# GRU, attention and AUGRU on one core: five shrinking softmax blocks, two products moved from VectorE to GpSimd, attention matmuls ahead of the next gates, first loads reordered

## The chip, the cores and the metric

The kernel runs on one core of a Trainium2 chip. The metric is device time in microseconds (us) of that core, the median of several executions. "Faster" or "slower" is said of a difference above 2%.

## The reference

A recommender scores 1024 users. Each has 100 history items of 128 numbers. A GRU runs over the history, an attention network scores each GRU state against the candidate item, the softmax of the scores pools the states, and the pooled vector (its element t, not a score) weights step t of a second recurrence, the AUGRU. A small network predicts from its last state and other features.

```python
h_new = (1 - z) * n + z * h                     # GRU, 100 steps; keys = all states
feat  = concat([keys, q, keys - q, q * keys])   # q: the item's embedding
score = mlp(feat)                               # 512 -> 80 -> 40 -> 1, relu
attn  = softmax(where(mask == 1, score, -inf), over the 100 steps)
pooled = einsum('bt,btd->bd', attn, keys)
# AUGRU over the keys: u = pooled[:, t] * sigmoid(...), h = (1 - u) * h + u * h_hat
# cut: history sum, predictor
```

## The kernel before

The batch is cut into two halves of 512 columns; half 1 runs five steps ("ticks") behind half 0. A tile is 128 x 512 in fp32 (256 KB). A step of a half has six gate matmuls and three for the attention (three layers, working on three different steps); the profile shows two instructions for each, 18 in all. Scores are collected row by row; at the end of a block (`ENDS`) the softmax of the block is made, and the rows of that block can be pooled: a row is one step's weights broadcast over the partitions, `eb`, times the key tile `k`, added to `pooled`.

```python
ENDS = (48, 92, T)
# gates of step t: matmuls into PSUM, then a chain on VectorE and ScalarE
nc.vector.scalar_tensor_tensor(out=u, in0=ph, scalar=bhh[:, 2:3], in1=r, op0=ALU.add, op1=ALU.mult)
nc.vector.tensor_add(pi, pi, u)
nc.scalar.activation(pi, pi, AF.Tanh, bias=bih[:, 2:3])
nc.vector.tensor_sub(d, h if t else h0, pi)
nc.vector.tensor_mul(d, pz, d)
nc.vector.tensor_add(hn, pi, d)                 # the new state
nc.gpsimd.tensor_mul(m, x, m)                   # history sum, on GpSimd
nc.gpsimd.tensor_add(hist[:, cols], hist[:, cols], m)
nc.sync.dma_start(out=keys_d[t][:, cols], in_=hn)
# ... attend(t): three pairs of matmuls
nc.vector.tensor_mul(kq, self.h, item[:, self.cols])
# ... pm = wk.h + wkq.kq + w12.mv, then f = pm + q0, mv = relu(f)
# ... pool(count): for each row
eb = kp.tile([P, HB], F32, name="eb")           # kp: 4 buffers of each tile
nc.sync.dma_start(out=eb, in_=e_d[j][row, self.cols].partition_broadcast(P))
k = kp.tile([P, HB], F32, name="k")
nc.sync.dma_start(out=k, in_=keys_d[t][:, self.cols])
nc.vector.tensor_mul(eb, k, eb)                 # the pooling product
nc.vector.tensor_add(acc, acc, eb)              # the sum; acc = pooled[:, cols], in SBUF
# ... the loop over ticks
for half, s in now:
    if 0 <= s < T: half.gru(s)                  # AUGRU steps from T + GAP on: cut
for half, s in now:
    if 0 <= s < T:
        half.attend(s)
        half.pool(2 if len(half.todo) > T - s else 1)
```

All big loads go through one queue (SyncE's). In PSUM the kernel keeps six tiles for gates (`ps`) and two for attention (`pa`); each is called a bank here. Independent instructions are reordered before they reach an engine, so the order on an engine isn't the program's.

## Time and profile before

| | before |
|---|---|
| median of 3 runs | 2873.81 us (2870.04 to 2875.78) |
| profiled span, granted clock | 2876.6 us, 0.972 |
| TensorE / VectorE / GpSimd busy | 93% / 64% / 28% |
| pooling sums: number, mean | 198, 767 ns |

The page's first part gives busy time of each engine; its second cuts the span into 40 slices and gives the busy tenths of each (9 is 90% or more).

```profile
PE 2669.4 (93%) x6080; PEld 1150.3 (40%) x6080; DVE 1843.4 (64%) x2674; ACT 945.5 (33%) x1431; POOL 809.9 (28%) x615
...
PE   6999999999999988999998847499999999999998
...
DVE  4666666666678998766666988655555555555553
...
POOL 3333333333333332333332300022222222222221
```

TensorE (PE) has three weak places: the first slice, two slices of 8 where VectorE (DVE) is at 9, and the hole of 8, 8, 4, 7, 4. The hole is the turn, where GRU and pooling end and the AUGRU begins.

To compare kernels I cut the span into five stages and count TensorE's instructions. The view below gives, for each stretch, its length, then busy us and (instructions) of TensorE, its weight loads, VectorE, ScalarE and GpSimd, then granted clock, DMA share and GB/s.

```profile
0.00:80.00 80.00, 56.55 (x106) 22.60 (x106) 39.11 (x56) 18.47 (x28) 30.25 (x35) 0.89 0.58 185
80.00:720.00 640.00, 620.83 (x1424) 267.38 (x1425) 412.69 (x556) 205.70 (x317) 214.74 (x159) 1.00 0.30 98
720.00:1520.00 800.00, 761.93 (x1732) 324.81 (x1731) 602.78 (x857) 252.26 (x388) 264.83 (x190) 0.99 0.48 152
1520.00:1920.00 400.00, 280.78 (x619) 118.70 (x618) 302.30 (x481) 99.81 (x150) 70.28 (x52) 0.85 0.65 206
1920.00:2870.00 950.00, 946.38 (x2199) 416.40 (x2198) 486.54 (x726) 367.68 (x549) 229.84 (x181) 1.00 0.31 98
```

At the full pitch of 0.429 us an instruction, **lost time** of a stage is its length minus 0.429 x its instructions: start 80 - 106 x 0.429 = 35 us, steady GRU 29, softmax and pooling stages (720 to 1520) 57, turn (1520 to 1920) 134. This measure is used throughout. It is not idle time alone: where instructions take longer than the pitch, that counts as lost too.

### The profile page before, as it was taken

What the parts mean: (1) busy time and instruction counts of PE and PEld (TensorE: products, weight loads), DVE (VectorE), ACT (ScalarE), POOL (GpSimd) and SP (SyncE); (2) the same over time, 40 slices, a digit from 0 to 9 for tenths busy, and PEclk for the clock granted to TensorE, in tenths of its full rate; (3) what the DMA queues carried; (4) which work ended last, traced back from release to release, by engine and by line L of the source; (5) the groups of instructions that cost most, each with busy time, mean ns of one, the idle gap of its engine ahead of it and who ended that gap; (6) DMA issues with size and microseconds to landing.
All of it is one profiled execution on the core that took longest, in us unless ns stands there. A gap on an engine that the chain in (4) does not pass through costs nothing.

```text
span 2876.6 us, 22338 instructions
## 1 busy us (share of the span) xinstructions
PE 2669.4 (93%) x6080; PEld 1150.3 (40%) x6080; DVE 1843.4 (64%) x2674; ACT 945.5 (33%) x1431; POOL 809.9 (28%) x615
## 2 busy tenths in 40 slices
PE   6999999999999988999998847499999999999998
PEld 2444444444434333444443312144444444444443
DVE  4666666666678998766666988655555555555553
ACT  2333333333333222333333312133333333333333
POOL 3333333333333332333332300022222222222221
PEclk8999999999999999999999978699999999999999
DMA  6332323222245777433334777733333333333331
GB/s 196 99 99 95 103 95 103 93 99 99 96 135 188 236 240 224 158 100 102 106 100 134 237 237 253 227 102 103 102 103 102 102 102 102 102 102 102 103 101 42
DMA packets 213650, 375.69 MB, mean 131 GB/s; under 512 B 31568, under 2 KB 32436, under 8 KB 213524
## 3 DMA queue, kind: packets, MB, share of 16 engines
q1 hardware_dynamic: 213524, 374.27, 40.9%
q8 instruction: 47, 0.77, 0.1%
q14 instruction: 79, 0.65, 0.1%
HBM read 320.08 MB, written 53.67 MB: 130 GB/s over the span
## 4 chain that ended last, share of the span: by engine, by line
PE 64%; DVE 20%; DMA 8%; issue 5%; ACT 3%; SPq 1%; POOL 1%; DVEq 0%; ACTq 0%; POOLq 0%
PE ps L189 18%; PE pm L237 10%; PE pu L348 6%; PE pr L348 6%; PE ph L348 6%; PE pr L350 6%; PE ph L350 6%; PE pu L350 6%; DVE d L218 3%; DMA k<-keys_d 3%; DVE hn L219 3%; DVE eb L318 3%; DMA eb<-e_d 3%; DVE u L209 2%; DVE d L217 2%
## 5 line engine op out<-in xcount | busy, mean ns | idle before, releaser
L189 PE MATMUL ps<-x,wih 128*128 128x512 f32 x1200 | 586.9, 597 | 0.0
L189 PE MATMUL ps<-hn,whh 128*128 128x512 f32 x1188 | 584.3, 599 | 1.8 <-DVE hn L219 1.8
L220 POOL TENSOR_TENSOR m<-x,m 128x512 f32<-128x512 f32 x200 | 262.7, 1313 | 1085.9 <-DMA x<-in_hist_x 1054.3
L362 POOL TENSOR_TENSOR u<-u,at 128x512 f32<-128x512 f32 x200 | 254.3, 1272 | 877.1 <-ACT u L361 865.1
L366 DVE TENSOR_TENSOR ph<-ph,hn 128x512 f32<-128x512 f32 x198 | 138.4, 699 | 450.5 <-ACT ph L364 450.3
L189 PEld LDWEIGHTS ps<-x,wih 128*128 128x128 f32 x1200 | 230.1, 192 | 291.3 <-issue 282.2
L189 PEld LDWEIGHTS ps<-hn,whh 128*128 128x128 f32 x1188 | 228.3, 192 | 289.9 <-issue 286.9
L237 PE MATMUL pm<-hn,wk 128*128 128x512 f32 x400 | 219.7, 632 | 95.0 <-DVE hn L219 94.8
L243 ACT ACTIVATE mv<-f 128x512 f32<-128x512 f32 x204 | 128.5, 630 | 540.9 <-DVE f L241 531.6
L221 POOL TENSOR_TENSOR hist<-hist,m 128x512 f32<-128x512 f32 x200 | 287.6, 1438 | 15.7
L215 ACT ACTIVATE ps<-ps,bih 128x512 f32<-128x512 f32 x200 | 132.4, 662 | 423.1 <-DVE ps L214 423.0
L348 PE MATMUL pr<-k,wr 128*128 128x512 f32 x396 | 203.4, 595 | 46.6 <-DMA k<-keys_d 46.6
L209 DVE SCALAR_TENSOR_TENSOR u<-ps,bhh,r 128x512 f32<-128x512 f32 x198 | 147.5, 745 | 144.6 <-PE ps L189 138.0
L237 PE MATMUL pm<-kq,wkq 128*128 128x512 f32 x400 | 216.5, 624 | 11.6 <-DVE kq L231 11.0
L241 DVE TENSOR_TENSOR f<-pm,q 128x512 f32<-128x512 f32 x204 | 139.7, 685 | 132.2 <-PE pm L237 132.0
L357 ACT ACTIVATE pr<-pr,br 128x512 f32<-128x512 f32 x198 | 131.1, 662 | 276.1 <-PE pr L350 276.1
L237 PE MATMUL pm<-mv,w 128*128 128x512 f32 x404 | 210.8, 604 | 2.6 <-ACT mv L243 2.6
L350 PE MATMUL pr<-hn,wr 128*128 128x512 f32 x396 | 204.1, 597 | 9.1 <-DVE hn L368 9.1
L217 DVE TENSOR_TENSOR d<-hn,ps 128x512 f32<-128x512 f32 x198 | 135.6, 685 | 115.1 <-ACT ps L215 115.1
L361 ACT ACTIVATE u<-pu,bu 128x512 f32<-128x512 f32 x200 | 137.3, 687 | 214.6 <-PE pu L350 214.6
L348 PE MATMUL pu<-k,wu 128*128 128x512 f32 x400 | 205.2, 594 | 0.0
L350 PE MATMUL ph<-r,wh 128*128 128x512 f32 x396 | 202.7, 593 | 2.4 <-DVE r L358 2.4
(93 smaller groups left out, 2936.5 us busy)
## 6 DMA issues: line engine op xcount, KB each, us to landing
k<-keys_d SPq DMA_DIRECT2D x400, 256.0 KB
eb<-e_d SPq DMA_DIRECT2D x206, 256.0 KB
x<-in_hist_x SPq DMA_DIRECT2D x200, 256.0 KB
m<-mask_d SPq DMA_DIRECT2D x200, 256.0 KB
keys_d<-hn SPq DMA_DIRECT2D x200, 256.0 KB
at<-att_d SPq DMA_DIRECT2D x200, 256.0 KB
s_b<-mv SPq DMA_DIRECT2D x200, 2.0 KB
item<-in_item SPq DMA_DIRECT2D x1, 512.0 KB
```

Source lines behind the costliest of these rows:

```text
L189: nc.tensor.matmul(p, lhsT=w[:, g, :], rhs=v, start=(n == 0), stop=(n == len(parts) - 1),)
L209: nc.vector.scalar_tensor_tensor(out=u, in0=ph, scalar=bhh[:, 2:3], in1=r, op0=ALU.add, op1=ALU.mult)
L217: nc.vector.tensor_sub(d, h if t else h0, pi)
L220: nc.gpsimd.tensor_mul(m, x, m)
L221: nc.gpsimd.tensor_add(hist[:, cols], hist[:, cols], m)
L237: nc.tensor.matmul(p, lhsT=w, rhs=v, start=(n == 0), stop=(n == len(parts) - 1))
L241: nc.vector.tensor_add(f, p, q0[:, self.cols])
L348: nc.tensor.matmul(p, lhsT=w[:, 1, :], rhs=k, start=True, stop=v is None)
L350: nc.tensor.matmul(p, lhsT=w[:, 0, :], rhs=v, start=False, stop=True)
L361: nc.scalar.activation(u, pu, AF.Sigmoid, bias=later["bu"])
L362: nc.gpsimd.tensor_mul(u, u, at)
L366: nc.vector.tensor_sub(ph, ph, h)
```

## The change

The intent: more, shrinking blocks so that few rows are left for the turn; the rows spread evenly; VectorE relieved of two products; each state used later, so that TensorE need not wait for it; an earlier start.

```diff
-ENDS = (48, 92, T)
+ENDS = (44, 72, 88, 96, T)
 # first loads: x of step 0 goes second in the queue, whh behind the biases
+    x_first = xp.tile([P, HB], F32, name="x")
+    nc.sync.dma_start(out=x_first, in_=a["hist_x"][0][:, :HB])
 # buffers: xp 5 -> 6, kp 4 -> 5
 # the two reciprocals of 128x512 become one of 128x8, through DRAM
-                nc.vector.tensor_mul(kq, self.h, item[:, self.cols])
+                nc.gpsimd.tensor_mul(kq, self.h, item[:, self.cols])
-                    nc.vector.tensor_mul(eb, k, eb)
+                    nc.gpsimd.tensor_mul(eb, k, eb)
                     nc.vector.tensor_add(acc, acc, eb)
 # the loop: attention of the step before, then the gates, half by half
-        for half, s in now: ... half.gru(s)
-        for half, s in now: ... half.attend(s)
-                half.pool(2 if len(half.todo) > T - s else 1)
+        for half in halves:
+            if 1 <= s <= T:
+                half.attend(s - 1)
+            if 0 <= s < T:
+                half.gru(s, parts)
+                left = next(e for e in ENDS if e > s - 2) - s + 2
+                half.pool(-(-len(half.todo) // left))
 # cut: functions split so that a step could be done in parts (it is done in one)
```

More of the change, by code (lines that the diff above doesn't have):

```diff
@@ L65 @@
     att_d = dram.tile([T, B], F32, name="att_d")
+    rlen_d = dram.tile([P, NG], F32, name="rlen_d")
     def load(name, shape, src=None, dt=F32):
@@ L73 @@
     wih = load("wih", [P, 3, P])
-    whh = load("whh", [P, 3, P])
+    xp = ctx.enter_context(tc.tile_pool(name="xp", bufs=6))
+    x_first = xp.tile([P, HB], F32, name="x")
+    nc.sync.dma_start(out=x_first, in_=a["hist_x"][0][:, :HB])
     bih = load("bih", [P, 3])
     bhh = load("bhh", [P, 3])
+    whh = load("whh", [P, 3, P])
     pre = ctx.enter_context(tc.tile_pool(name="pre", bufs=1))
@@ L120 @@
     y = const.tile([1, B], F32, name="y")
-    xp = ctx.enter_context(tc.tile_pool(name="xp", bufs=5))
     hp = ctx.enter_context(tc.tile_pool(name="hp", bufs=8))
@@ L125 @@
     sp = ctx.enter_context(tc.tile_pool(name="sp", bufs=2))
-    kp = ctx.enter_context(tc.tile_pool(name="kp", bufs=4))
+    kp = ctx.enter_context(tc.tile_pool(name="kp", bufs=5))
     ps = ctx.enter_context(tc.tile_pool(name="ps", bufs=6, space=PSUM))
@@ L159, in load_later @@
             later[n] = load(n, shape)
-        len_i = pre.tile([P, B], I32, name="len_i", tag="once2")
-        nc.sync.dma_start(out=len_i, in_=a["len_i"].partition_broadcast(P))
-        length = const.tile([P, B], F32, name="length")
+        len_i = pre.tile([T, B], I32, name="len_i", tag="once2")
+        nc.sync.dma_start(out=len_i, in_=a["len_i"].partition_broadcast(T))
+        length = const.tile([T, B], F32, name="length")
         nc.vector.tensor_copy(length, len_i)
         later["length"] = length
+        len_g = pre.tile([P, NG], I32, name="len_g")
+        nc.sync.dma_start(out=len_g, in_=a["len_i"].rearrange("(p g) -> p g", p=P))
+        rlen_g = pre.tile([P, NG], F32, name="rlen_g")
+        nc.vector.tensor_copy(rlen_g, len_g)
+        nc.vector.reciprocal(rlen_g, rlen_g)
+        nc.sync.dma_start(out=rlen_d, in_=rlen_g)
     class Half:
@@ L174, in __init__, with gru @@
             self.todo = []
-        def gru(self, t):
+        def gru(self, t, parts):
             cols = self.cols
-            x = xp.tile([P, HB], F32, name="x")
-            nc.sync.dma_start(out=x, in_=a["hist_x"][t][:, cols])
+            if t or self.i:
+                x = xp.tile([P, HB], F32, name="x")
+                nc.sync.dma_start(out=x, in_=a["hist_x"][t][:, cols])
+            else:
+                x = x_first
             m = xp.tile([P, HB], F32, name="m")
@@ L184, in gru, with gru_chain @@
             hn = hp.tile([P, HB], F32, tag="h", name="hn")
+            for c in parts:
+                self.gru_chain(t, x[:, c], h[:, c] if t else h0[:, c], hn[:, c])
+            nc.gpsimd.tensor_mul(m, x, m)
+            nc.gpsimd.tensor_add(hist[:, cols], hist[:, cols], m)
+            nc.sync.dma_start(out=keys_d[t][:, cols], in_=hn)
+            self.h = hn
+        def gru_chain(self, t, x, h, hn):
+            n = x.shape[-1]
             def gate(g, parts):
-                p = ps.tile([P, HB], F32, tag="g", name=f"ps{g}")
-                for n, (w, v) in enumerate(parts):
+                p = ps.tile([P, n], F32, tag="g", name=f"ps{g}")
+                for j, (w, v) in enumerate(parts):
                     nc.tensor.matmul(
@@ L192, in gate @@
                         rhs=v,
-                        start=(n == 0),
-                        stop=(n == len(parts) - 1),
+                        start=(j == 0),
+                        stop=(j == len(parts) - 1),
                     )
@@ L199, in gru @@
             pr = gate(0, both)
-            r = wp.tile([P, HB], F32, name="r")
+            r = wp.tile([P, n], F32, tag="r", name="r")
             nc.scalar.activation(r, pr, AF.Sigmoid, bias=brz[:, 0:1])
@@ L206, in gru @@
             nc.scalar.activation(pz, pz, AF.Sigmoid, bias=brz[:, 1:2])
-            u = wp.tile([P, HB], F32, name="u")
+            u = wp.tile([P, n], F32, tag="u", name="u")
             if t:
@@ L215, in gru @@
             nc.scalar.activation(pi, pi, AF.Tanh, bias=bih[:, 2:3])
-            d = wp.tile([P, HB], F32, name="d")
-            nc.vector.tensor_sub(d, h if t else h0, pi)
+            d = wp.tile([P, n], F32, tag="d", name="d")
+            nc.vector.tensor_sub(d, h, pi)
             nc.vector.tensor_mul(d, pz, d)
             nc.vector.tensor_add(hn, pi, d)
-            nc.gpsimd.tensor_mul(m, x, m)
-            nc.gpsimd.tensor_add(hist[:, cols], hist[:, cols], m)
-            nc.sync.dma_start(out=keys_d[t][:, cols], in_=hn)
-            self.h = hn
         def attend(self, t):
@@ L326, in weights @@
                 out=att,
-                in0=later["length"][:T, self.cols],
+                in0=later["length"][:, self.cols],
                 scalar=step[:T, :],
@@ L333, in weights, with augru, augru_chain @@
             nc.sync.dma_start(out=att_d[:, self.cols], in_=att)
-        def augru(self, t):
+        def augru(self, t, parts):
             cols = self.cols
-            wr, wu, wh = later["wr"], later["wu"], later["wh"]
-            at = kp.tile([P, HB], F32, name="at")
-            nc.sync.dma_start(out=at, in_=att_d[t, cols].partition_broadcast(P))
-            k = kp.tile([P, HB], F32, name="k3")
-            nc.sync.dma_start(out=k, in_=keys_d[t][:, cols])
-            h = self.h if t else None
-            hn = hp.tile([P, HB], F32, tag="h", name="hn3")
+            at = kp.tile([P, HB], F32, name="at", bufs=4)
+            nc.sync.dma_start(out=at, in_=att_d[t, cols].partition_broadcast(P))
+            k = kp.tile([P, HB], F32, name="k3", bufs=4)
+            nc.sync.dma_start(out=k, in_=keys_d[t][:, cols])
+            hn = hp.tile([P, HB], F32, tag="h", name="hn3")
+            for c in parts:
+                h = self.h[:, c] if t else None
+                self.augru_chain(k[:, c], at[:, c], h, hn[:, c])
+            self.h = hn
+        def augru_chain(self, k, at, h, hn):
+            wr, wu, wh = later["wr"], later["wu"], later["wh"]
+            n = k.shape[-1]
             def gate(w, v, name):
-                p = ps.tile([P, HB], F32, tag="g", name=name)
+                p = ps.tile([P, n], F32, tag="g", name=name)
                 nc.tensor.matmul(p, lhsT=w[:, 1, :], rhs=k, start=True, stop=v is None)
@@ L353, in augru @@
             r = None
-            if t:
+            if h is not None:
                 pr = gate(wr, h, "pr")
-                r = wp.tile([P, HB], F32, tag="r", name="r3")
+                r = wp.tile([P, n], F32, tag="r", name="r3")
                 nc.scalar.activation(pr, pr, AF.Sigmoid, bias=later["br"])
@@ L359, in augru @@
             pu = gate(wu, h, "pu")
-            u = wp.tile([P, HB], F32, tag="u", name="u3")
+            u = wp.tile([P, n], F32, tag="u", name="u3")
             nc.scalar.activation(u, pu, AF.Sigmoid, bias=later["bu"])
@@ L364, in augru @@
             nc.scalar.activation(ph, ph, AF.Tanh, bias=later["bh"])
-            if t:
+            if h is not None:
                 nc.vector.tensor_sub(ph, ph, h)
@@ L370, in augru @@
                 nc.vector.tensor_mul(hn, u, ph)
-            self.h = hn
         def features(self):
             cols = self.cols
-            rlen = wp.tile([P, HB], F32, name="rlen")
-            nc.vector.reciprocal(rlen, later["length"][:, cols])
-            nc.vector.tensor_mul(hist[:, cols], hist[:, cols], rlen)
+            rlen = kp.tile([P, HB], F32, tag="eb", name="rlen")
+            nc.sync.dma_start(
+                out=rlen,
+                in_=rlen_d.rearrange("p g -> (p g)")[cols].partition_broadcast(P),
+            )
+            nc.gpsimd.tensor_mul(hist[:, cols], hist[:, cols], rlen)
             cross = const.tile([P, HB], F32, name=f"cross{self.i}")
@@ L423, in predict @@
             )
+    parts = (ts(0, HB),)
     halves = [Half(i) for i in range(NH)]
-    for tick in range(2 * T + GAP + LAG):
+    for tick in range(2 * T + GAP + LAG + 1):
         if tick == 2:
             load_later()
-        now = [(half, tick - LAG * half.i) for half in halves]
-        for half, s in now:
-            if 0 <= s < T:
-                half.gru(s)
-            elif T + GAP <= s < 2 * T + GAP:
-                half.augru(s - T - GAP)
-        for half, s in now:
-            if 0 <= s < T:
-                half.attend(s)
-                half.pool(2 if len(half.todo) > T - s else 1)
-            elif s == T:
+        for half in halves:
+            s = tick - LAG * half.i
+            if 1 <= s <= T:
+                half.attend(s - 1)
+            if s == T:
                 half.attend(T)
                 half.attend(T + 1)
+            if 0 <= s < T:
+                half.gru(s, parts)
+            elif T + GAP <= s < 2 * T + GAP:
+                half.augru(s - T - GAP, parts)
+            if 0 <= s < T:
+                left = next(e for e in ENDS if e > s - 2) - s + 2
+                half.pool(-(-len(half.todo) // left))
+            elif s == T:
                 half.pool(len(half.todo))
@@ L445 @@
                 half.features()
-            elif s == 2 * T + GAP - 1:
+            elif s == 2 * T + GAP:
                 half.predict()
```

## The prediction

> **What bounds the kernel now.** I read the page's first two parts, then busy time by stage, then the waits of TensorE, then the timeline inside each stage. On the page TensorE is busy 93%. The same page's slices show that this is an average over stages, so I cut the span at the places where slices or DMA rate change. The columns of the next view are: stretch and its length, then busy us (and instructions) of TensorE, its weight loads, VectorE, ScalarE and GpSimd, then granted clock, DMA share, GB/s.
>
> ```profile
> 72.00:790.00 718.00, 696.85 (x1599) 299.79 (x1598) 464.57 (x625) 232.00 (x357) 241.23 (x179) 1.00 0.30 98
> 790.00:900.00 110.00, 102.46 (x243) 43.83 (x241) 76.27 (x112) 38.56 (x57) 34.69 (x26) 0.98 0.39 126
> 900.00:1200.00 300.00, 272.63 (x597) 113.59 (x597) 274.92 (x396) 84.14 (x134) 94.95 (x65) 0.97 0.72 229
> 1200.00:1520.00 320.00, 318.64 (x737) 138.04 (x737) 205.28 (x288) 107.13 (x164) 110.68 (x82) 1.00 0.33 101
> 1520.00:1900.00 380.00, 260.78 (x573) 109.91 (x572) 292.14 (x466) 92.23 (x138) 65.20 (x48) 0.85 0.67 212
> 1900.00:2840.00 940.00, 940.00 (x2191) 415.10 (x2190) 485.63 (x725) 366.54 (x547) 229.86 (x181) 1.00 0.32 102
> ```
>
> Count matmuls rather than busy time. The AUGRU stage runs without a gap: 940 us / 2191 = 0.429 us each. At that pitch the instructions of each stage need a known time, and the remainder is lost: start (0 to 72, 89 instructions) 34 us; 72 to 790: 718 - 1599 x 0.428 = 34; 790 to 900: 6; 900 to 1200: 300 - 255 = 45; 1200 to 1520: 5; 1520 to 1900: 380 - 245 = 135; 1900 to 2840: 2; the end: 11. The sum is about 271 us, and about 2606 us is matmul work that this change does not reduce. So the change can win from 271 us and no more, and half of that lies in one stage, the turn from GRU to AUGRU. Who holds TensorE up:
>
> ```profile
> PE pm L237 <- DVE hn L219: 94.8, 72, 17.5
> PE pr L348 <- DMA k<-keys_d: 46.6, 1, 46.6
> PE pm L237 <- DVE kq L231: 11.0, 19, 1.8
> ...
> PE pt L264 <- DMA s_b<-mv: 8.3, 1, 8.3
> ```
>
> (waited in total, times, longest.) The attention matmul waits for the state just made: 22.8 us in 45 waits between 72 and 890, 22.1 in 16 waits between 900 and 1200, and 36.2 in 6 waits in the turn. The AUGRU's first key load waits 46.6 us in one piece. In a steady GRU tick (300 to 316 us) the order is gates of half 0, gates of half 1, attention of half 0, attention of half 1; the period is 16.2 us where 36 instructions need 15.4, and the pause sits ahead of the second attention.
>
> VectorE is 92% busy from 900 to 1200 (274.92 of 300), where the first 96 pooling rows are worked off, at two VectorE operations each. It is the rate setter there. One line of the timeline says something more:
>
> ```profile
> 32.38 3.34 DVE L377 RECIPROCAL rlen<-length 128x512 f32<-128x512 f32 x1
> ```
>
> This reciprocal belongs to tick 114 by the program, and it runs at 32 us. So instructions are not issued in the program's order: independent work is pulled forward as soon as its inputs exist. That is bad here (the two reciprocals, 3.34 us each, hold the state of step 1 back), and it warns me that an "even" pooling rate in the program may not be even on the chip: the old rate of one row per half and tick shows as a burst of 96 rows in 300 us.
>
> **What the Trainium skill says.** (1) "SBUF — State Buffer", Who interferes with whom: a VectorE instruction with two SBUF inputs and a GpSimd instruction that reads SBUF exclude each other, and the second blocks. The trace agrees: kq (two SBUF inputs) has a minimum of 622 ns and a median of 691, but 1.45 and 1.52 us where it starts beside the GpSimd product of line 220. Its mean is 959 ns. The gate operations have an input in PSUM and stay at 685 to 697. (2) "GPSIMD Engine Reference", Elementwise — side-by-side cycle accounting: a two-input product costs GpSimd about 2.6 cycles per element, so 512 x 2.6 / 1.2 GHz = 1.11 us as an estimate. The trace has 1.26 to 1.31 us (lines 362 and 220) and decides. (3) "TensorE: Matmul & The Clock Gate", its table of specifications: VectorE, ScalarE and GpSimd have strict FIFO queues. A product that waits for its load therefore holds up all that stands behind it; the timeline near 1000 us, where VectorE stops 1.10 us on `eb<-e_d`, is in keeping with it.
>
> **Part by part.**
>
> *Attention ahead of the gates.* The state of a half is now used after the other half's nine matmul pairs, 18 x 0.429 = 7.7 us later. After the last gate the chain is about 0.70 + 0.66 + 3 x 0.69 us plus hops, some 4 us. The wait should go: of 34 + 5 us lost outside pooling I leave 8. Gain 30.
>
> *kq on GpSimd.* VectorE loses 2 x 0.96 us a tick, GpSimd gains 2 x 1.27. GpSimd per tick: 2 x (1.31 + 1.27 + 1.27) = 7.7 of 15.4 us. There is room, and contention outside pooling ends. The product adds 1.3 us plus queueing ahead of the second attention pair, in a slack of 7.7 - 4 us. I count 0.
>
> *Pooling product on GpSimd.* Per row VectorE drops from 0.79 + 0.77 to 0.77 (perhaps 1.4 when locked out), GpSimd takes 1.3. At the burst rate of about 5 rows a tick: VectorE 2 x 4.2 + 5 x 0.77 to 1.4 = 12 to 15.5 us, GpSimd 7.7 + 6.5 = 14.2. TensorE becomes the bound again, narrowly. Before, 96 rows in the GRU cost 51 us (6 + 45), 0.53 each. After, about 180 rows fall into it; at half the rate, 0.28 each, that is 50 us. Gain 0, but it pays for the next part.
>
> *Five blocks.* Before, half the rows came too late: by the program 45 rows of each half are still undone when its GRU ends (4 + 45 from block two, less 14, plus 10), and the trace shows some 112 rows between 1550 and 1850. After, by the same count, 10 rows remain (4 from block four, 4 + 2 from block five). Turn, worked out anew: half 1 runs five steps alone, 5 x 8.2 = 41 us; half 0 meanwhile needs three attention layers (7), score to row (2), softmax with table load (7), its round trip to DRAM (5), 10 rows (15), weights and their round trip (5), about 45 us in all. Then half 0 runs AUGRU alone, at 6.9 us a step (the period at the tail, 2831 to 2852), while half 1 does the same. In all about 91 us with 5 x 7.7 + 6 x 5.1 = 69 us of work, so 22 lost; I allow 40 for queues. Gain 95. The single key wait of 46.6 us goes with it, as that load stood behind the pooling loads in the one load queue.
>
> *Four more softmaxes* (two blocks, two halves): transposes of 0.2 to 0.3 us, 16 a softmax at most beside other work, two table loads of 1.28, and TensorE waits like the 8.3, 3.1 and 4.0 of before. About 3 us lost each, plus 6 us of transposes. Loss 18.
>
> *First loads and reciprocal.* The first gate ran at 12.2 us, behind the query product, and the second state came at 36.3, held up by the reciprocals. With x second in the queue and the reciprocals shrunk to 128x8, the chain alone allows a step about every 9 us. But GpSimd's first kq may stand behind the first mask product, which waited for its row until 15.4 us. Of 34 us lost I leave 18. Gain 16. The end stays as it is (+2).
>
> Sum: 2874 - 30 - 0 - 0 - 95 + 18 - 16 + 2 = 2749. A second way, by ticks: start and five lone steps 60, 95 double ticks of 15.43 = 1466, softmax and pooling stalls 70, turn 91 to 100, 94 double AUGRU steps of 10.29 = 967, tail and predictor 53 gives 2707 to 2716. I take 2735, between them.
>
> **Rivals.** *A: GpSimd takes over as the brake.* In a burst it is 90% busy, in order, and every pooling product waits for two loads. If one is late, kq stands behind it, and TensorE behind kq; the sum on VectorE stands behind the product too. For: VectorE idled 43 us before line 318 waiting for loads, and the wait moves to GpSimd rather than going. Against: loads have five buffers now, at 0.72 DMA share there is some room. Cost 0.3 us more a row: about 2790. *B: the turn hardly shortens*, because a chain of softmax, DRAM round trips and single queues, not rows, holds it. For: 9 and 8.3 us waits of that sort. Against: VectorE was 77% busy and TensorE waited 17.5 us on a state while rows ran ahead of it. It would give about 2800. *C: all goes well*, rows cost nothing extra and the start gains fully: about 2670.
>
> **Range and chances.** Prediction 2735 us; 8 in 10 between 2670 and 2800. To be within 2% it would have to stay above 2816, which needs A and B together: 0.06. Slower needs a new stall of 190 us: 0.01.
>
> **What would show it.** Right: TensorE's waits on hn L219 fall from 95 us to under 20; the key wait of 46.6 us is gone; the stretch with under 90% TensorE around the turn shrinks from about 340 us to about 120; VectorE's share in pooling falls below 85% and GpSimd's rises above 75%; steady ticks are 15.4 to 15.6 us. Wrong: waits of attention matmuls for kq on GpSimd above 40 us (A), a turn still longer than 200 us (B), pooling sums near 1.4 us with a VectorE still 90% busy, or the second state still later than 30 us.

## The result

The changed kernel takes 2892.87 us (median of 4, 2890.72 to 2901.52); the kernel before took 2872.53 us on the same chip (2870.04 to 2875.78; a fourth run joined the three of the table above). The ratio is 1.0076 (95% interval 1.0052 to 1.0099): within 2%, and slightly slower. A ratio is the mean time of one kernel's fast runs over the mean of the other's of the same rounds, so not quite the ratio of the medians. Executions over 1.5% slower than the fastest of the same kernel are left out of the means. The result is correct.

The page after, the same lines:

```profile
PE 2693.2 (93%) x6112; PEld 1162.2 (40%) x6112; DVE 1639.4 (57%) x2318; ACT 954.2 (33%) x1443; POOL 1304.2 (45%) x1015
...
PE   6999999999898879988889896899999999999998
...
DVE  3555555555676555565766576655555555555553
...
POOL 4444444544668664464865664522222222222221
```

The hole at the turn has shrunk to one slice of 6, but TensorE now has 7s and 8s all the way from slice 11, while VectorE and GpSimd are at 4 to 8 there. The same stages:

```profile
0.00:80.00 80.00, 53.64 (x93) 20.88 (x94) 24.16 (x45) 15.76 (x24) 36.09 (x40) 0.85 0.61 191
80.00:720.00 640.00, 636.78 (x1490) 281.80 (x1489) 352.64 (x504) 221.15 (x334) 313.03 (x249) 1.00 0.31 103
720.00:1520.00 800.00, 698.24 (x1523) 292.12 (x1523) 504.58 (x664) 219.01 (x343) 507.43 (x384) 0.95 0.54 173
1520.00:1920.00 400.00, 342.48 (x776) 144.98 (x775) 264.68 (x371) 124.68 (x187) 215.78 (x160) 0.94 0.50 158
1920.00:2870.00 950.00, 950.00 (x2214) 419.02 (x2213) 488.49 (x729) 368.85 (x551) 230.59 (x182) 1.00 0.32 100
```

| lost us | start | steady | softmax and pooling | turn | sum |
|---|---|---|---|---|---|
| before | 35 | 29 | 57 | 134 | 255 |
| after | 40 | 1 | 147 | 67 | 255 |

So 28 us were won in the steady GRU and 67 in the turn, and 90 were lost in the pooling stage and 5 at the start. The end loses 13 us in both. The 13 us between the two profiled spans are the 32 transposes that four more softmaxes need (32 x 0.429 = 13.7; a transpose takes 0.2 to 0.3 us, less than a pitch, so some of that is waiting around them).

In the stage that lost 90 us no engine is full: VectorE is busy 504.58 of 800 us, GpSimd 507.43, DMA 0.54. It is a matter of waiting, then. Of the 147 us TensorE is idle for 102; in the other 45 its instructions took longer than the pitch, at a granted clock of 0.95 (before: 38 and 19, at 0.99). TensorE's waits and those of VectorE and GpSimd for one another (total, times, longest):

```profile
DVE pooled L337 <- POOL eb L336: 157.4, 86, 5.5
...
POOL kq L249 <- DVE hn L241: 100.2, 42, 10.5
...
PE pm L255 <- DVE hn L241: 87.0, 39, 10.8
POOL eb L336 <- DMA k<-keys_d: 76.4, 48, 4.9
...
PE pm L255 <- POOL kq L249: 56.0, 47, 6.0
...
PE pt L282 <- DMA s_b<-mv: 9.2, 7, 2.7
```

The key wait of 46.6 us is gone, but the attention's wait for the state is 87.0 us after 94.8, and 56.0 us of waits for `kq`, now on GpSimd, have joined it. VectorE's sums wait 157.4 us for GpSimd's products. And the sum itself has become longer. The first line of each of the next fences is what one line of the kernel did: duration in ns as min/median/max, first and last start. Before:

```profile
L319 DVE TENSOR_TENSOR pooled<-pooled,eb x198: 661/682/1773, 815.0 to 1838.7; 128x512 f32<-128x512 f32 x198
```

After:

```profile
L337 DVE TENSOR_TENSOR pooled<-pooled,eb x198: 674/1434/1774, 727.3 to 1860.2; 128x512 f32<-128x512 f32 x198
```

The same instruction has nearly the same minimum and maximum, but its median goes from 682 to 1434 ns; the mean from 767 to 1211. The timeline of the changed kernel shows why a state comes late (start, duration, engine, line, operation; in brackets the idle time before it and what ended it):

```profile
888.21 0.69 DVE L241 TENSOR_TENSOR hn<-ps,d 128x512 f32<-128x512 f32 x1
...
889.04 1.27 POOL L249 TENSOR_TENSOR kq<-hn,item 128x512 f32<-128x512 f32 x1 [1.49 <-DVE hn L241]
...
889.41 1.45 DVE L337 TENSOR_TENSOR pooled<-pooled,eb 128x512 f32<-128x512 f32 x1
...
893.29 2.49 POOL L336 TENSOR_TENSOR eb<-k,eb 128x512 f32<-128x512 f32 x2
...
894.59 1.74 DVE L337 TENSOR_TENSOR pooled<-pooled,eb 128x512 f32<-128x512 f32 x1 [3.72 <-POOL eb L336]
...
896.25 0.74 DVE L231 SCALAR_TENSOR_TENSOR u<-ps,bhh,r 128x512 f32<-128x512 f32 x1
...
899.18 1.24 DVE L337 TENSOR_TENSOR pooled<-pooled,eb 128x512 f32<-128x512 f32 x1
...
901.06 0.69 DVE L241 TENSOR_TENSOR hn<-ps,d 128x512 f32<-128x512 f32 x1
...
901.80 0.70 PE L255 MATMUL pm<-hn,wk 128*128 128x512 f32 x1 [2.78 <-DVE hn L241]
```

Two states are 12.85 us apart (888.21 to 901.06), where 18 instructions need 7.7. Two things are to be seen. VectorE stands 3.72 us before a sum, since the product it needs starts only at 893.29 on GpSimd. And when the sum comes, it runs beside the second of two products (the two take 893.29 to 895.78) and takes 1.74 us in place of 0.68; `u`, the next link of the state's chain, has to wait for it. The first sum, beside `kq`, takes 1.45, and the last, which stands between two links of the chain, 1.24.

### The profile page after: what moved, and what is told of

The parts are those of the page before. It is cut to its first block, busy times and chain, and to the rows that moved or that the text cites. A ratio compares the mean times of both kernels' runs of the same rounds, so it can differ in the third digit from the quotient of the medians.

```text
span 2889.7 us, 22623 instructions
## 1 busy us (share of the span) xinstructions
PE 2693.2 (93%) x6112; PEld 1162.2 (40%) x6112; DVE 1639.4 (57%) x2318; ACT 954.2 (33%) x1443; POOL 1304.2 (45%) x1015
## 4 chain that ended last, share of the span: by engine, by line
PE 39%; DMA 5%; DVE 5%; POOL 4%; issue 3%; ACT 1%; SPq 1%; POOLq 0%; DVEq 0%; ACTq 0%
PE pu L372 6%; PE ph L374 6%; PE pr L372 6%; PE ph L372 6%; PE pr L374 6%; PE pu L374 6%; PE ps L211 2%; DVE pooled L337 2%; POOL eb L336 2%; DMA eb<-e_d 1%; DMA k<-keys_d 1%; PE pm L255 1%; DMA x<-in_hist_x 1%; POOL kq L249 1%; POOL m L200 1%
## 5 line engine op out<-in xcount | busy, mean ns | idle before, releaser
L337 DVE TENSOR_TENSOR pooled<-pooled,eb 128x512 f32<-128x512 f32 x198 | 239.5, 1211 | 159.4 <-POOL eb L336 157.4
L336 POOL TENSOR_TENSOR eb<-k,eb 128x512 f32<-128x512 f32 x198 | 273.1, 1392 | 107.4 <-DMA k<-keys_d 76.4
L249 POOL TENSOR_TENSOR kq<-hn,item 128x512 f32<-128x512 f32 x200 | 261.5, 1307 | 109.2 <-DVE hn L241 100.2
L255 PE MATMUL pm<-kq,wkq 128*128 128x512 f32 x400 | 230.4, 660 | 56.0 <-POOL kq L249 56.0
L201 POOL TENSOR_TENSOR hist<-hist,m 128x512 f32<-128x512 f32 x200 | 259.7, 1299 | 14.0
L255 PE MATMUL pm<-mv,w 128*128 128x512 f32 x404 | 224.1, 638 | 1.6 <-ACT mv L261 1.6
L372 PE MATMUL ph<-k,wh 128*128 128x512 f32 x400 | 204.4, 592 | 0.0
```

The source lines that it names most:

```text
L249: nc.gpsimd.tensor_mul(kq, self.h, item[:, self.cols])
L255: nc.tensor.matmul(p, lhsT=w, rhs=v, start=(n == 0), stop=(n == len(parts) - 1))
L336: nc.gpsimd.tensor_mul(eb, k, eb)
L372: nc.tensor.matmul(p, lhsT=w[:, 1, :], rhs=k, start=True, stop=v is None)
```

## The experiments

Two theories of the 90 us:

- **Crossed queues.** VectorE, in order, stands behind GpSimd's product; GpSimd, in order, has `kq` behind products and loads. The waits (157.4 us, 56.0 us) are the loss.
- **Exclusion.** The sum has two SBUF inputs, GpSimd reads SBUF, and they shut each other out. The longer sums sit in the state's chain and are the loss; the waits are harmless.

The expectations call crossed queues Theory 1 and exclusion Theory 3; their Theory 2 is the smaller claim that `kq` merely comes late for TensorE.

Timed runs have four executions, three of them in rounds against the kernel before; ratios are to that. Kernels of different calls ran on different chips, so I compare them by ratio (1% is 28.7 us). "Lost" is worked out as above.

| run | median us | ratio, 95% interval | lost: start / pooling / turn | sums' mean ns |
|---|---|---|---|---|
| after | 2892.87 | 1.0076 (1.0052 to 1.0099) | 40 / 147 / 67 | 1211 |
| e1 | 2855.63 | 0.9936 (0.9917 to 0.9955) | 30 / 128 / 66 | 1151 |
| e2 | 2804.78 | 0.9766 (0.9743 to 0.9789) | 39 / 77 / 50 | 874 |
| e3 | 2828.57 | 0.9850 (0.9823 to 0.9878) | 27 / 108 / 56 | 825 |
| e4 | 2884.99 | 1.0039 (1.0021 to 1.0058) | 28 / 130 / 91 | on GpSimd |
| e5 | 2920.84 | 1.0191 (1.0171 to 1.0212) | 28 / 163 / 87 | on GpSimd |
| e6 | 2932.91 | 1.0233 (1.0210 to 1.0256) | 39 / 153 / 103 | 1058 |
| e7 | 2888.86 | 1.0079 (1.0057 to 1.0101) | 41 / 135 / 73 | 1067 |
| e8 | 2817.60 | 0.9834 (0.9814 to 0.9853) | 40 / 96 / 44 | 684 |
| e9 | 2892.91 | 1.0067 (1.0051 to 1.0083) | 39 / 143 / 71 | 1236 |
| e10 | 2825.94 | 0.9835 (0.9818 to 0.9851) | 40 / 95 / 43 | 697 |
| e11 | 2795.18 | 0.9728 (0.9703 to 0.9753) | 26 / 82 / 45 | 874 |
| e12 | 2865.56 | 0.9977 (0.9956 to 0.9998) | 34 / 83 / 125 | 749 |
| e13 | 2768.06 | 0.9660 (0.9641 to 0.9679) | 26 / 58 / 39 | 687 |
| e14 | 2850.36 | 0.9941 (0.9917 to 0.9964) | 26 / 80 / 121 | 839 |
| e15 | 2970.57 | 1.0368 (1.0349 to 1.0386) | 34 / 115 / 158 | 1076 |
| e16 | 2917.02 | 1.0156 (1.0139 to 1.0173) | 31 / 87 / 156 | 696 |

### Undoing one product or both: e1, e2, e3

```diff
 e1 and e3
-                nc.gpsimd.tensor_mul(kq, self.h, item[:, self.cols])
+                nc.vector.tensor_mul(kq, self.h, item[:, self.cols])
 e2 and e3
-                    nc.gpsimd.tensor_mul(eb, k, eb)
+                    nc.vector.tensor_mul(eb, k, eb)
```

> The changed kernel with kq = h*item back on VectorE; the pooling product stays on GpSimd. Theory 1 (crossed queues: GpSimd's kq waits for VectorE's state, VectorE's pooling sum waits for the GpSimd product that stands behind that kq): one of the two crossings is gone, VectorE's wait for the product falls from 157 us to under 90, the stretch 680 to 1520 loses about half as much; 2830 to 2855 us. Theory 2 (kq is merely late for TensorE: 56 us of waits): the 56 us go and little else changes; 2835 to 2850, but VectorE's wait for the product stays near 157. Theory 3 (GpSimd and VectorE exclude each other[...]): kq joins those that are locked out, no gain; 2880 to 2910. All: the start gets some 10 to 15 us shorter, as kq no longer stands behind the mask products.

> The changed kernel with the pooling product back on VectorE; kq stays on GpSimd. Theory 1: no wait of VectorE on GpSimd is left, the pooling stages lose what VectorE's load makes them lose, like before (0.5 us a row or less, as kq is off VectorE): 2790 to 2830 us. Theory 2: kq still waits in GpSimd's queue, though behind less; TensorE's waits for kq stay above 30 us; 2840 to 2880. Theory 3: GpSimd has less, VectorE more instructions with two inputs in SBUF; about as now, 2870 to 2900.

> Both products back on VectorE; what remains of the change is the five blocks, the order and the loads. Theory 1: no engine waits across, but VectorE is full in the pooling stages: 2780 to 2830 us, the gains of the steady stage (26 us) and of the turn (68 us) stand alone against before, less some 25 us for four more softmaxes. Theory 2: the same, 2790 to 2830. Theory 3: 2830 to 2870.

With the pooling product back on VectorE (e2) the ratio falls from 1.0076 to 0.9766, 89 us; VectorE does two operations a row again and is busier (639.54 of 800 us in the pooling stage, after 504.58), and still TensorE loses 77 us there in place of 147. That is the opposite of what a count of busy time says. The sums fall to 874 ns, while TensorE's waits for `kq` stay (55.2 us after 56.0). Putting `kq` back alone (e1) wins 40 us, some 10 of them at the start. But with the product on VectorE, `kq` is better on GpSimd: e3 is 24 us slower than e2. Counted from e3, `kq` on GpSimd wins 24 us, the product there costs 25 (e1), and both together cost 65: the two moves aren't additive.

Of the expectations, Theory 3 missed its range in all three runs (in e3 by 1 us), and Theory 1 had e2 and e3 in its range, e1 within 1 us of it, and the fall of VectorE's wait in e1 right (89.4 us, under 90), but not that the stage would lose half as much (128 us after 147). So these three runs speak for crossed queues, if for either; the next had to part the two.

### The sum on GpSimd too: e4, e5

e4 has product and sum on GpSimd (no queue crosses within a row) and `kq` on VectorE; e5 also issues the score rows from ScalarE's queue.

```diff
-                    nc.vector.tensor_add(acc, acc, eb)
+                    nc.gpsimd.tensor_add(acc, acc, eb)
 e5 only
-            nc.sync.dma_start(out=self.s_b[s - a0 : s - a0 + 1, :], in_=mv[SC : SC + 1, :])
+            nc.scalar.dma_start(out=self.s_b[s - a0 : s - a0 + 1, :], in_=mv[SC : SC + 1, :])
```

> Product and sum of pooling both on GpSimd, kq on VectorE: VectorE never waits for a pooling row. GpSimd needs 5.2 us a tick plus 2.6 us a row. Theory 1: TensorE's waits in the pooling stages nearly vanish, GpSimd runs pooling in the background; 2740 to 2800 us. Theory 3 or plain capacity of GpSimd: rows pile up, the turn becomes long as in the kernel before, or kq is locked out by a GpSimd that is never idle: 2850 to 2950.

> The run before with product and sum on GpSimd took 2885 us although TensorE was at 40 of 40 us while GpSimd was 97% busy; it lost in front of the softmax transposes instead (136 us of waits in 9 pieces), which wait for the score rows, whose copies stand in the one load queue behind loads that wait for GpSimd. Here the same kernel issues the 200 score-row copies from ScalarE's queue. If the load queue is what held the transposes, these waits fall below 40 us and the time to 2760 to 2800. If GpSimd's capacity is the brake, the rows pile up at the end of the GRU all the same: 2850 or more.

Between 840 and 920 us of e4 TensorE runs without a gap (x187 in 80 us) while GpSimd is busy 77.73 of 80 us: a full GpSimd doesn't brake TensorE as long as nothing of TensorE's stands behind the rows. Yet e4 wins little (1.0039, in the range given for Theory 3 or a GpSimd at its capacity). As I read it, GpSimd is now too slow for the rows and the one load queue fills up: TensorE's softmax transposes `pt` wait 136 us in all, in few long pieces of up to 30.3 us, put down to loads of x, of scores and of masks. e5 was to remove that wait. It did (to some 31 us), and was slower still, 1.0191: it missed the 2760 to 2800 us, and only the other branch, 2850 or more, has its time. ScalarE sat idle 162.1 us ahead of `r` after 14.7 in e4, 64 of them put down to loads, so the copies in its queue seem to have held it (not tested alone); VectorE waited 365 us for `r` after 252, and TensorE 115.3 us for states after 35.4. These two tell nothing for or against exclusion; they show that the rows' place is not free on any engine.

### Less waiting behind the product: e6, e7

e6 holds each sum back until two later products have been issued. e7 ties the rows of a half's tick behind its new state on VectorE and its history sum on GpSimd, so that they run at a more even pace (9 to 18 sums in each 80 us from 720 to 1520, where the changed kernel has 0 to 25).

```diff
 e6
-                    nc.vector.tensor_add(acc, acc, eb)
+                    # issued two rows later, ordered after that row's product
 e7
-                half.pool(-(-len(half.todo) // left))
+                with tc.issue_after(half.last), tc.issue_after(half.last_pool):
+                    half.pool(-(-len(half.todo) // left))
```

> The changed kernel with each pooling sum issued two rows behind its product; same engines, same work, same buffers. Theory 1 (crossed queues): VectorE's wait for the product (157 us) falls below 60, the pooling stages lose at most half: 2800 to 2850 us. Theory 3 (the two engines exclude each other): VectorE's waits turn into longer sums, nothing gained: 2870 to 2900. Rival: with two sums owed, three of five buffers remain for loads, so the loads come later and pooling slows: the wait moves to GpSimd's loads, 2860 to 2890.

> The changed kernel with the pooling rows of a tick really queued behind that tick's state, so that the program's pace is the chip's pace (at most 2, later 3 rows for each half and tick rather than bursts of 5 to 6 a tick). Theory 1: with fewer rows in a tick and the sums behind the state instead of ahead of it, the waits of VectorE for products fall below 70 us and the recurrence is spared: 2800 to 2840. Theory 3: the number of products and sums that meet is the same, so 2870 to 2900.

The waits of VectorE for products fell from 157.4 us to 36.9 (e6) and 32.7 (e7), and neither kernel got faster: 1.0233 and 1.0079. Theory 1 missed both times; e6 lies above every range given, e7 in that of Theory 3. The waits of e6 show where the time went:

```profile
POOL eb L340 <- DMA eb<-e_d: 203.3, 81, 7.7
...
PE pm L257 <- POOL kq L251: 145.9, 61, 7.2
...
DVE pooled L347 <- POOL eb L340: 36.9, 10, 7.9
...
PE pm L257 <- DVE hn L243: 15.9, 5, 8.7
```

As I read it, a held sum holds its buffer, so the next load is late (products waited 23.7 us for `eb` loads in the changed kernel, 203.3 here), and `kq` stands behind the waiting product. In e7 the wait moved in the same way, from the state (23.2 us) to `kq` (129.2 us). So crossed queues are real, but these two ways of taking VectorE's side of them away won nothing. That alone doesn't refute Theory 1, as both made new waits.

### The exclusion by itself: e8, its control e9, and a correct version e10

e8 gives the sum one SBUF input: `eb` plus a tile of zeros that lies in PSUM. It computes a wrong result on purpose (the comparison passed it all the same, so it doesn't feel this term, and "correct" says little of the pooled sum in the other runs either; e8 is no candidate). As the zeros take a PSUM bank, e9 has the zeros and five gate banks but the sum of the changed kernel. e10 is correct: the accumulators lie in PSUM, with five gate banks and one attention bank left.

```diff
 e8 and e9
-    ps = ... bufs=6
+    ps = ... bufs=5        # and a PSUM tile zero, set to 0
 e8
-                    nc.vector.tensor_add(acc, acc, eb)
+                    nc.vector.tensor_add(acc, eb, zero)
 e10
-    pooled = const.tile([P, B], F32, name="pooled")
+    pooled = [po.tile([P, HB], F32, name=f"pooled{i}") for i in range(NH)]   # PSUM
-    ps bufs=6, pa bufs=2
+    ps bufs=5, pa bufs=1
```

> Wrong result on purpose: the pooling sum adds a zero tile in PSUM instead of the running sum, so it has one input in SBUF and should not exclude GpSimd; one gate bank fewer (5) pays for the tile. Theory 3 (exclusion[...] makes the loss): sums fall from a mean of 1.21 us to 0.70, products from 1.39 to 1.27, and the time to 2800 to 2830. Theory 1: sums shorten as well, but VectorE's waits for products stay above 110 us: 2850 to 2880. The missing bank may cost something; a run with five banks alone follows if it matters.

> Control for e8: the changed kernel with one gate bank fewer and nothing else. If e8 was faster because its sums have a single SBUF input, this kernel must show the sums at about 1210 ns again and a time at or above the changed kernel's, 2885 to 2930 us. If e8 was faster because of the other bank number and the order of instructions that came with it, this one is near 2820 us too.

> A correct counterpart of e8: the changed kernel with the pooled accumulators in PSUM (two banks; five gate banks and one attention bank are left), so that the sum is again acc + product, with one SBUF input. Exclusion theory: sums at about 690 ns, 2800 to 2860 us although two banks are gone. Rival, that e8 won because its sum did not chain on the accumulator: sums above 1000 ns or a time near 2890 us.

The sums of e9:

```profile
L340 DVE TENSOR_TENSOR pooled<-pooled,eb x198: 674/1444/1783, 728.5 to 1859.4; 128x512 f32<-128x512 f32 x198
```

and of e8, with what VectorE waited for ahead of them:

```profile
L340 DVE TENSOR_TENSOR pooled<-eb,zero x198: 673/687/690, 727.1 to 1785.1; 128x512 f32<-128x512 f32 x198
...
its engine sat idle before it (us, times) until:
  POOL eb L339: 186.6, 109
```

And e10, number and mean of its sums from the page:

```profile
L338 DVE TENSOR_TENSOR pooled<-pooled,eb 128x512 f32<-128x512 f32 x198 | 138.0, 697 | 179.1 <-POOL eb L337 178.7
```

In e8 not one of 198 sums is longer than 690 ns once it has a single SBUF input. From e9 to e8 the ratio falls by 0.0233, 67 us; e9 is where the changed kernel is, so the bank isn't the reason. And VectorE's waits for products **rise**, to 186.6 us, in a kernel 67 us faster: the length of that wait doesn't measure the loss. (Nor does the name of a wait: in e9, as slow as the changed kernel, TensorE waits 21.3 us for states, 33.6 for `kq` and 82.2 for `d`, a link of the state's chain; the last falls to 52.9 in e8.) e10 has 0.9835, the same gain, with the sum kept and one more bank gone. All three expectations of exclusion held. Taking the exclusion away alone shows its share: in the pooling stage 143 us are lost in e9, 96 in e8 and 95 in e10, and in the turn 71, 44 and 43. So it makes about half (47 us) of the 90 us that the pooling stage had lost, and costs another 27 us in the turn.

### The parts alone: e12, e14, e15, e16

e12 is the kernel before with the new order of attention and gates. e15 is the kernel before with the pooling product on GpSimd, one word changed; e16 is e15 with the accumulators in PSUM as in e10. e14 is e11, the version told of in the next part, with three blocks in place of five.

```diff
 e12: the loop of the diff above, with gru(s) and the old pooling rate
 e14, from e11
-ENDS = (44, 72, 88, 96, T)
+ENDS = (48, 92, T)
 e15, from the kernel before
-                    nc.vector.tensor_mul(eb, k, eb)
+                    nc.gpsimd.tensor_mul(eb, k, eb)
 e16, from e15: pooled in PSUM, ps bufs=5, pa bufs=1
```

> The kernel before with the attention matmuls put ahead of the gates and no other part. Theory of the prediction: 30 us gained outside pooling, so about 2843 us (2830 to 2855), with the attention's waits for the state falling from 95 us to under 50; pooling stages and the turn as before. Rival, that the gain needs kq on GpSimd or is lost again in the pooling stages where VectorE is full: 2860 to 2880 us.

> The version of 2795.2 us with the three softmax blocks of before (48, 92, 100) in place of five, to price the blocks by themselves. The prediction's terms (95 won in the turn, 18 lost on four softmaxes) say 2795 + 77 = 2872; I allow 2845 to 2875 us, with some 110 us or more lost between 1520 and 1880 in place of 44. Rival, that rows pulled ahead of the turn cost there what they save in it: 2785 to 2815 us.

> The kernel before with the pooling product moved to GpSimd and no other part. The prediction had VectorE as the rate setter of the pooling stage, so it should win most of the 41 us lost there between 880 and 1200: 2830 to 2845 us, sums staying near 770 ns. Exclusion theory: sums rise to 1.1 us or more, which takes back half of what VectorE gives away and delays the state as well, so 2860 to 2890 us.

> e15 (the kernel before with the pooling product on GpSimd, 2970.6 us) with the pooled accumulators in PSUM, one SBUF input for the sum, one gate bank and one attention bank fewer. If the exclusion of sum and GpSimd makes most of e15's loss of about 105 us: sums at 690 ns and 2860 to 2905 us. If GpSimd's slower product and the sum's wait behind it make it (1.38 us a row in the turn, where VectorE alone did both in about 1.6): sums at 690 ns too, but 2930 to 2970 us, with the turn as long as in e15.

**e12** wins only 0.2% (6 to 7 us). The steady stage loses 0 us in place of 29, as predicted, but the wait for the state stays at 87.8 us where under 50 was expected, and the pooling stage 83 in place of 57: there VectorE's wait of the pooling product for `eb` loads went from 14.6 us (880 to 1200 us) to 53.0; what TensorE had won was given back. The rival's range (2860 to 2880) held.

**e14** against e11 prices the blocks: ratio 0.9941 against 0.9728, 61 us. The turn loses 121 us with three blocks and 45 with five; the pooling stage 80 and 82; the transposes cost up to 14. The expectation (2845 to 2875) held.

**e15** fits neither theory's range. One product moved to GpSimd makes the kernel before 3.7% slower, 106 us. Its sums have a mean of 1076 ns after 767 and wait 118.9 us for products, which themselves wait 156.7 us for loads; the pooling stage loses 58 us more, the turn 24, and the rows spill over the end of the turn (12 us lost after 1920 in a stretch, up to 2600, where the kernel before loses none). **e16** bounds the share of the exclusion: without it the ratio is 1.0156, so 0.0212 of 0.0368 goes, 61 us of 106; it lies between the two ranges given. But 13 of the 61 are won between 80 and 720 us, ahead of the first sum (795.8), so by the banks or the order of instructions, and e16 has no control with the banks alone. The stages in which sums run lose 43 us less, and that is what the exclusion can account for here. At least 45 us stay, with sums of 696 ns: the slower product (1.31 us where VectorE needs some 0.8), the crossed queues and two banks fewer are what is left to name; no run here parts these three.

### Versions built on this: e11, e13

e11 is e2 with `kq` on VectorE in the first 12 steps, since in e2 as in the changed kernel `kq` stands behind the mask products on GpSimd at the start. e13 is e11 with the accumulators in PSUM.

```diff
-                nc.gpsimd.tensor_mul(kq, self.h, item[:, self.cols])
+                eng = nc.vector if t < 12 else nc.gpsimd
+                eng.tensor_mul(kq, self.h, item[:, self.cols])
 # and the pooling product on nc.vector; e13: pooled in PSUM, ps bufs=5, pa bufs=1
```

> Pooling product back on VectorE as in e2 (2804.8 us), and kq on VectorE in the first 12 steps only, to take it out from behind the mask products at the start. Theory: the first 80 us hold about 117 matmuls in place of 95, worth 22 x 0.43 = 9 us, so 2790 to 2800 us, and nothing changes after 200 us. Rival, that the start is made up for later by waits: about 2805 us.

> The best version so far (product on VectorE, kq on VectorE in the first 12 steps, 2795.2 us) with the pooled accumulators in PSUM, so that the sum has one SBUF input. Exclusion theory: the sums fall from 874 to about 700 ns, 198 x 0.17 = 34 us less on VectorE, of which TensorE gets up to 20: 2775 to 2795 us. Rival: with the product still locked out against kq and two banks gone there is nothing to win, 2795 to 2815 us.

e11 takes 2795.18 us, within its range; its start loses 26 us in place of 39. e13 takes 2768.06 us, 3.4% faster than the kernel before and the best of all. That is 7 us better than the range expected, on a chip where the kernel before was 7 us faster as well; by ratio it lies at the range's edge. Its pooling stage and turn:

```profile
720.00:1520.00 800.00, 751.68 (x1730) 324.27 (x1729) 623.52 (x906) 250.99 (x389) 377.82 (x284) 0.99 0.60 193
1520.00:1920.00 400.00, 363.28 (x841) 155.68 (x840) 254.17 (x412) 141.46 (x210) 106.62 (x83) 0.97 0.45 141
```

58 and 39 us are lost. The pooling stage loses what it lost before the change, with 150 sums in it where the kernel before had 87, and the turn loses 39 where it lost 134. VectorE is busy 623.52 of 800 us, more than in the changed kernel (504.58), and TensorE is faster. From e10 (95 us lost in the pooling stage) to e13 (58) the product went back to VectorE and the early `kq` with it; as I read it, the other part of the changed kernel's loss is the product's own slowness and the `kq` behind it, which the runs don't part further.

## Why the prediction was wrong

It said 2735 us, 2670 to 2800, and, by its chances for the rest, 0.93 for faster by over 2%; the change is 0.8% slower. Its sum has a slip: 2874 - 30 - 95 + 18 - 16 + 2 is 2753, not 2749. Two readings were loose: 900 to 1200 us holds 82 sums, not 96 rows, and of the gate operations `u` takes 744 ns, not 685 to 697.

- **Where the time was lost, and that half of it was the turn: right.** The stages with the lost time were the ones that moved.
- **Five blocks, gain 95, less 18 for softmaxes: near.** In the changed kernel the turn loses 67 us in place of 134, so 67 won, not 95; part of the rest is again the product on GpSimd (45 in e11). By themselves, e14 against e11, the blocks are worth 61 us net where 77 were predicted. The key wait of 46.6 us went, as said; but TensorE's stretch under 90% did not shrink to about 120 us: of the twelve slices of 40 us from 1400 to 1880 only two reach 90%.
- **Attention ahead of the gates, gain 30: right in its stage, wrong in the sum.** 28 us were won from 80 to 720 us, and the period of a tick became 640 / (1490 / 36) = 15.46 us, within the 15.4 to 15.6 named. But the wait for `hn` is 87.0 us, not under 20, as it came back in the pooling stage, and e12 shows that the part alone gives its gain back there.
- **`kq` on GpSimd, 0: mis-sized because it depends on the next part.** It costs 40 us with the pooling product on GpSimd (e1), and is worth 24 without it (e3 against e2).
- **First loads, gain 16: wrong by 21.** The start lost 5 us more, though the second state was done at 24.5 us, earlier than the 30 named. The doubt in the prediction, `kq` behind the mask products, was the cause: e11 takes it away and the start loses 26, so 9 won of the 16.
- **Pooling product on GpSimd, gain 0 with 50 us lost: the step that failed.** The prediction's sentence was "TensorE becomes the bound again, narrowly." It added busy times ("0.77 to 1.4" for the sum among them), found 12 to 15.5 us a tick on VectorE and 14.2 on GpSimd, about the 15.4 of TensorE or less, and concluded that the stage loses less per row. No engine was full, as it said: VectorE 63%, under the 85 named, GpSimd 63% where over 75 was named. But the two engines don't add up separately. A sum that met a GpSimd instruction took up to 1.8 us (the median of all is 1.43), and it stands in one queue with the state's chain. The lock was cited and its size read (1.45 us), yet it was put into a throughput and not into the latency from one state to the next. The stage lost 147 us; without the exclusion 95 (e10), with the product back on VectorE 77 (e2).

Of the rivals, A (GpSimd as brake) showed its sign, 56.0 us of waits for `kq`, above the 40 named; its cost was set at 55 us. It has a part, as `kq` off GpSimd wins 40 us (e1), but the larger part was another: GpSimd isn't full, it shuts VectorE out. "Pooling sums near 1.4 us with a VectorE still 90% busy" came half true: 1.43 us in the median, with VectorE 63% busy. The full VectorE wasn't needed for the harm. The chances were too sure: "within 2%", which came, had 0.06 and was said to need A and B together, but 90 us lost in one stage were enough to cancel all that was won.

The stages explain the miss: predicted lost time was 18 at the start, 8 + 50 + 18 in steady, pooling and softmaxes, 40 in the turn, together 134; measured 255. Those 121 us and the transposes carry 2753 to about 2885.

The Trainium skill had what was needed. "SBUF — State Buffer", Who interferes with whom, says that a VectorE instruction with at most one SBUF input, outside the performance modes that use two ports, does not contend with GpSimd; e8 agrees (maximum 690 ns). "Perfetto Trace Analysis", Optimizing Scalar/DVE Operations, warns that offloading operations between VectorE and GpSimd "might not help". Here it did harm: 106 us in e15.

## What to carry to other kernels

Before moving an elementwise operation from VectorE to GpSimd, list which VectorE operations with two SBUF inputs will run beside it, and ask whether one of them stands in the queue of the critical recurrence: the cost is then up to their lengthening times their number, even if both engines end up half idle (here 0.55 us x 198 = 109 us more on VectorE in e9 than in e8, of which 67 reached the kernel's time). If the move is wanted, give those operations an operand in PSUM (an accumulator is a natural one). And take the wait that ends a chain, not the largest wait in the table: here a wait of 157 us could be cut to 33 for nothing, and grew to 187 in a kernel 67 us faster.

## What the Trainium skill lacked or had wrong

- "Perfetto Trace Analysis", Optimizing Scalar/DVE Operations, says that "a 2-port DVE op" holds the shared read port as a lock and that offloading "might not help", but not that a plain two-input sum is such a case, nor that the move can do harm. A sum of 128x512 fp32 with both inputs in SBUF suffers: median 682 ns before, 1434 ns with the product on GpSimd, 687 with one input in PSUM; the move alone cost 106 us (e15).
- "SBUF — State Buffer", Who interferes with whom, has the rule but not this remedy or its worth: an accumulator in PSUM won 0.0232 of the time, 67 us, over the control with five gate banks although it took one bank more (e10 against e9), and e13 against e11 some 20 us with the product on VectorE.
- "GPSIMD Engine Reference", Elementwise — side-by-side cycle accounting, gives 2.6 cycles an element, 1.11 us as an estimate for 512 elements; the product took 1.27 us in the median, and 1.39 in the mean beside VectorE's sums. The page's table names a dispatch for each instruction but gives no time for GpSimd's.
